# Biases on another queue, halves inverted singly, one more piece summed on TensorE: both ends of a norm-attention kernel

## The chip, the cores and the metric

One core of one Trainium2 chip runs the whole program. The metric is the device time of one execution in microseconds (us). The median of six runs of the kernel before is 1860.31 us (1860.1 to 1861.24).

## The reference

The input `x` is 32 images of 256 channels on 32 by 32 positions, in float32. Each image is group-normed (32 groups of 8 channels), projected to q, k and v, put through attention with 8 heads of 32 channels over the 1024 positions with a strictly causal mask, and added to `x`:

```python
def _L0_conv_ref(x, q_w, q_b, kv_w, kv_b):
    xf = x.reshape(B, C, S)
    q = jnp.einsum('oc,bcs->bos', q_w, xf) + q_b[None, :, None]
    kv = jnp.einsum('oc,bcs->bos', kv_w, xf) + kv_b[None, :, None]
    ...
    mask = jnp.tril(jnp.ones((S, S), dtype=x.dtype), -int(MASK_CENTER))
    scores = jnp.einsum('bhqd,bhkd->bhqk', q, k) / jnp.sqrt(jnp.asarray(dk, x.dtype))
    scores = jnp.where(mask == 0, jnp.asarray(-10000.0, x.dtype), scores)
    attn = jax.nn.softmax(scores, axis=-1)
    attn = jnp.where(mask == 0, jnp.asarray(0.0, x.dtype), attn)
    out = jnp.einsum('bhqk,bhkd->bhqd', attn, v)
...
x = x + _L0_conv_ref(_gn(x), L0_conv_q_w, L0_conv_q_b, L0_conv_kv_w, L0_conv_kv_b)
```

## The kernel before, in words

The images ("batches", 0 to 31) are worked one after the other, all in float32. The 256 channels are two groups `g` of 128 partitions, and each group holds four heads. The 1024 positions are two halves `hf` of 512 columns. A batch so has four outputs of 128 by 512, which the code numbers n = 0 to 3 (n = 2 g + hf) and which I call its halves.

**Norm and projection.** `norm_channels`, `norm_mean`, `norm_deviation`, `norm_variance`, `norm_rstd` and `norm_apply` make the normed `xn`: statistics on VectorE (DVE), averages over the groups by small products on TensorE (PE), the power on GpSimd (POOL), and the subtraction and scaling of one half per call on DVE. `project_qk` multiplies on PE into a PSUM tile, and ScalarE (ACT) writes q or k with the bias `qk_bias` added (line 230). For q the bias has to be scaled first (line 565). `project_v` makes v without its bias, which is added at the very end.

**Visits.** Attention of a batch goes in N = 12 visits, six for each group. A visit is a pair of pieces: a piece `f[hf][k]` is one block of 128 keys against the queries of a half; `h[k, part]` is one against half of such queries. `scores` (line 297) makes the products of both pieces on PE into three PSUM tiles, ACT takes three exponentials into `e` and `eh` (lines 330 and 332), and POOL sets masked entries to zero (line 290). One visit later `values` (line 343) multiplies the exponentials with v into `acc` and, where `summed` is true, DVE adds them into the running total of the half (line 359). ACT copies the finished `acc` to `num` (line 362).

**Sums.** A total still has to be summed over the 128 partitions. For batches 0 to 29 that goes through DMAs that fold it. For the last two ("late") batches `sums` (line 409) does it with `sum_keys` on PE into `pd`, ACT copies `pd` to `den`, and a DMA writes four rows to the DRAM tile `sums`. For the last half of batch 31 some pieces skip the total: `sum_piece` (line 396) adds them into `pd` on PE, and `sum_total` adds the total of the rest.

**Inverting and finishing.** `gather` (line 432) reads the sums back into a tile `rows` spread over partitions, `check_sums` (line 439) marks on DVE whether they are in range, `invert` (line 445) takes the reciprocal on DVE, writes it to the DRAM tile `inverses` and reads it back, broadcast over the 32 channels of each head, into one tile `rb` for each half (line 453, allocated in line 459 with four buffers). `finish` (line 462) multiplies `num` with `rb`, adds the bias of v and `x` on DVE and sends the half out (line 470). `finish_aside` (line 472) does the same with two operations on POOL and one on ACT. Halves 2 and 3 of the last batch take no detour through DRAM: `check_here` (line 484) and `invert_here` (line 491) work on the sums where they are, and `end_last` (line 495) closes with half 3 in two parts.

**Order.** The loop in lines 618 to 637 runs over all visits `i`. For each it emits the scores of visit `i`, then the functions that `at[i]` holds, then the values of visit `i - 1`, then the functions of `after[i]`. (Where `i % 12` is 6, those of `at[i]` go between the exponentials of that visit.) `when` (line 530) puts a function into one of these lists; lines 584 to 617 do so for each batch, with `first = 12 b`. On PE, ACT, DVE and POOL the order is exactly the order of this code (`manual_schedule`, line 554). SyncE (SP), which issues nearly all DMAs, is not in that list: its order is the compiler's choice. Each engine and each queue of DMA issues works in its order, and waits there for whatever the next instruction needs.

**What sets the last batch's order.** Sums of halves 0 to 3 are made behind visits 3, 7, 9 and 12 (`SUMS`, line 549, and line 593). Batch 30 is finished behind visits 7, 7, 8 and 9 of batch 31 (`FINISH`, line 551), and its inverses are asked for in visit 4 (lines 603 to 606).

Of the kernel before, what the change touches and what calls it, by code (L numbers as in the profile page):

```python
# [17 lines left out]
P = 128  # L18
HD = 32
CPG = 8  # L20
HALF = 512
# [6 lines left out]
ROW = 64  # L28
# [3 lines left out]
def tile_norm_attention_residual(  # L32
# [19 lines left out]
    nc = tc.nc  # L52
    B, C, H, W = x.shape
    S = H * W
# [54 lines left out]
    def unshifted():  # L109
# [24 lines left out]
        def load_weights():  # L134
            for n, w in enumerate((q_w, kv_w[0:C], kv_w[C : 2 * C])):
                live["wn", n] = epool.tile([P, 4, HALFBANK], F32, tag="eh", bufs=4, name=f"wn_{n}")[:, :NG, :C]
                nc.sync.dma_start(out=live["wn", n], in_=w.rearrange("(o p) c -> p o c", p=P))
            nc.scalar.dma_start(out=qk_bias[:, 0, :], in_=q_b.rearrange("(g p) -> p g", p=P))
            nc.scalar.dma_start(out=qk_bias[:, 1, :], in_=kv_b[0:C].rearrange("(g p) -> p g", p=P))
            nc.scalar.dma_start(out=v_bias_col, in_=kv_b[C : 2 * C].rearrange("(g p) -> p g", p=P))  # L140

        def turn_weights(n):
            wn = live["wn", n]
# [64 lines left out]
        def norm_apply(b, cols):  # L208
            if cols.start == 0:
                live["xn", b] = work.tile([P, NG, S], F32, tag="xn", name=f"xn_{b}")  # L210
            mean, rstd = live["mean", b], live["rstd", b]
            for g in range(NG):
                nc.vector.tensor_scalar(
                    live["xn", b][:, g, cols], live["x", b][:, g, cols],
                    mean[:, g : g + 1], rstd[:, g : g + 1], ALU.subtract, ALU.mult,
                )
# [215 lines left out]
        def gather(b, ns):  # L432

            if ns.start == 0:
                live["rows", b] = small.tile([P, ROW], F32, tag="rows", name=f"rows_{b}")
            part = slice(ns.start * HD, ns.stop * HD)
            nc.sync.dma_start(out=live["rows", b][part], in_=spread_rows(live["sums", b])[part])

        def check_sums(b, ns):
            part = slice(ns.start * HD, ns.stop * HD)  # L440
            rows, ok = live["rows", b][part], in_range[part, :ROW]
            nc.vector.scalar_tensor_tensor(ok, rows, SUM_MIN, ok, ALU.is_ge, ALU.mult)  # L442
            nc.vector.scalar_tensor_tensor(ok, rows, SUM_MAX, ok, ALU.is_le, ALU.mult)  # L443

        def invert(b, ns):
            part = slice(ns.start * HD, ns.stop * HD)
            inv = small.tile([P, ROW], F32, tag="inv", name=f"inv_{b}_{ns.start}")
            nc.vector.reciprocal(inv[part], live["rows", b][part])  # L448
            live["inv", b] = dram.tile([4, 4, HALF], F32, tag="inv", name=f"inverses_{b}_{ns.start}")
            nc.sync.dma_start(out=spread_rows(live["inv", b])[part], in_=inv[part])  # L450
            by_half = live["inv", b] if b >= B - 2 else live["inv", b].rearrange("j n c -> n j c")
            for n in ns:
                nc.sync.dma_start(
                    out=inverses(b, n),
                    in_=by_half[n].unsqueeze(1).broadcast_to([4, HD, HALF]),
                )
# [27 lines left out]
        def check_here(n, ok):  # L484

            least = small.tile([P, 1], F32, tag="least", name=f"least_{n}")
            junk = small.tile([P, HALF], F32, tag="den", name=f"junk_{n}")
            nc.vector.tensor_scalar(junk, live["den", n], SUM_MIN, 1.0, ALU.is_ge, ALU.min, accum_out=least)  # L488
            nc.vector.scalar_tensor_tensor(ok, live["most", n], SUM_MAX, least, ALU.is_le, ALU.mult)
# [40 lines left out]
        def when(i, f, where=at):  # L530
            where.setdefault(i, []).append(f)
# [22 lines left out]
        with tc.manual_schedule(engines={ENG.PE, ENG.Activation, ENG.DVE, ENG.Pool}):  # L554


            load_weights()
            if B > 1:
                load(1)
            junk = small.tile([P, 1], F32, tag="most", name="junk")  # L560
            nc.scalar.activation(junk, ones, AF.Exp)
            keep_busy(11)
            for g in range(NG):
                norm_channels(0, g)
            nc.vector.tensor_scalar_mul(qk_bias[:, 0, :], qk_bias[:, 0, :], SCALE)
            norm_mean(0)
            keep_busy(3)
            norm_deviation(0)
            norm_variance(0)
            norm_rstd(0)  # L570
            for n in range(3):
                turn_weights(n)
            keep_busy(3)
            for hf in range(NH):
                norm_apply(0, slice(hf * HALF, (hf + 1) * HALF))
            units = projections(0)
            for n, f in zip((None, None, 0, 0, 0, 0) + PROJECT[6:], units):
                if n is None:
                    f()
                else:  # L580
                    when(n, f)
            if B > 1:
                prepare(1, (None, None, 0, 1, 2, 3, 3, 3))
            for b in range(B):
                first, last, late = b * N, b == B - 1, b >= B - 2
                if b >= 1:
                    for n, f in zip(PROJECT if not last else PROJECT[:-1] + (8,), projections(b)):
                        when(first + n, f)
                if b >= 2:
                    when(max(first - 2 * N + 6, 0), lambda b=b: load(b))  # L590
                    prepare(b, [first + n for n in PREPARE])
                for n in every:
                    v = first + (N if last and n == 3 else SUMS[n])
                    if late:
                        when(v, lambda b=b, n=n: sums(b, *divmod(n, NH)), after)
                    else:
                        when(v, lambda b=b, n=n: fold(b, n, 2 * HD), after)
                        when(v + 2, lambda b=b, n=n: fold(b, n, HD), after)
                        when(v + 4, lambda b=b, n=n: stack(b, n))
                if not last:  # L600
                    if not late:
                        when(first + N + 6, lambda b=b: sum_folded(b), after)
                    v = first + N + (2 if late else 8)
                    when(v, lambda b=b: gather(b, every))
                    when(v + 2, lambda b=b: check_sums(b, every))
                    when(v + 2, lambda b=b: invert(b, every))
                    for n in every:
                        when(first + FINISH[late][n], lambda b=b, n=n: finish(b, n), after)
                else:
                    when(first + N - 4, lambda b=b: gather(b, every[:2]))  # L610
                    when(first + N - 3, lambda b=b: check_sums(b, every[:2]))
                    when(first + N - 3, lambda b=b: invert(b, every[:2]))
                    when(first + N, lambda b=b: check_here(2, in_range[:, ROW : ROW + 1]))
                    when(first + N, lambda b=b: invert_here(b, 2, slice(0, HALF)))
                    when(first + N, lambda b=b: finish(b, 2))
                    for n in every[:2]:
                        when(first + N, lambda b=b, n=n: finish_aside(b, n), after)
            for i in range(B * N + 1):
                if i < B * N:

                    between = at.pop(i, ()) if i % N == 6 else ()
                    scores(i // N, *visits[i % N], between)
                for f in at.pop(i, ()):
                    f()
                for n, pc in enumerate(products[(i - 1) % N] if i else ()):

                    summed = i < B * N - 2 or (i == B * N - 2 and n == 0)
                    values((i - 1) // N, pc, summed)
                    if i == B * N:
                        sum_piece(B - 1, pc, stop=n == 1)  # L630
                        if n == 0:
                            sum_total(B - 1)
                if i == B * N - 1:
                    for n, pc in enumerate(products[N - 2] + products[N - 3][1:]):
                        sum_piece(B - 1, pc, start=n == 0)
                for f in after.pop(i, ()):
                    f()
            assert not at and not after
            outside = end_last(B - 1)
# [157 lines left out]
```

## Time and profile before

| what | value |
|---|---|
| median of six runs | 1860.31 us (1860.1 to 1861.24) |
| time of the profiled execution | 1860.07 us |
| its span, first to last instruction | 1858.0 us |
| granted TensorE clock, mean | 0.997 |
| busy ACT, share of the span | 1413.9 us, 76% |
| busy POOL, share of the span | 773.4 us, 42% |
| first projection on PE | 13.47 us after the start |
| issue of the last output DMA | 1853.56 us after the start |

The times in a line of the timeline are the start of a group of like instructions on one engine and the time that the group takes, in us from the start of the span; in brackets stands the idle time of that engine just before, and what ended it. "SPq" and "ACTq" are the queues that issue DMAs, "PEld" is the loading of weights on PE. The chain of waits gives start, time, engine, tile and line of the work that led to the end. A row of the stretch table gives start and end of a stretch, its length, then busy time (with the number of instructions) of PE, PEld, DVE, ACT and POOL, the granted clock of PE, the mean busy share of the sixteen DMA engines, and GB/s. A PE instruction in such a line is one pass; a product of float32 operands has two.

The stretches of the last batch by the scores of its visits: visit 4 starts at 1808.40 us, visit 8 at 1825.59, visit 11 at 1836.96. The last product of the attention ends at 1846.31 us.

### The profile page before, as it was taken

What the parts mean: (1) busy time and instruction counts of PE and PEld (TensorE: products, weight loads), DVE (VectorE), ACT (ScalarE), POOL (GpSimd) and SP (SyncE); (2) the same over time, 40 slices, a digit from 0 to 9 for tenths busy, and PEclk for the clock granted to TensorE, in tenths of its full rate; (3) what the DMA queues carried; (4) which work ended last, traced back from release to release, by engine and by line L of the source; (5) the groups of instructions that cost most, each with busy time, mean ns of one, the idle gap of its engine ahead of it and who ended that gap; (6) DMA issues with size and microseconds to landing.
All of it is one profiled execution on the core that took longest, in us unless ns stands there. A gap on an engine that the chain in (4) does not pass through costs nothing. (4 is left out here: it accounts for less than half of the span.)

```text
span 1858.0 us, 54181 instructions
## 1 busy us (share of the span) xinstructions
PE 1839.9 (99%) x23440; PEld 933.9 (50%) x23440; DVE 1555.9 (84%) x1601; ACT 1413.9 (76%) x1777; POOL 773.4 (42%) x743
## 2 busy tenths in 40 slices
PE   8999999999999999999999999999999999999997
PEld 5455555454554555545555545555455555454543
DVE  3778888888888888888888888888888888888868
ACT  5777777777777777777777777777777777777776
POOL 1443443434434444344344343443443443434314
PEclk9999999999999999999999999999999999999999
DMA  3447665676766676666767656767567666667412
GB/s 120 69 79 145 140 147 112 116 146 138 144 116 127 133 142 140 134 124 124 140 139 143 122 119 131 145 141 144 108 126 146 138 141 114 130 132 141 98 45 89
DMA packets 77517, 233.43 MB, mean 126 GB/s; under 512 B 19808, under 2 KB 20832, under 8 KB 61912
## 3 DMA queue, kind: packets, MB, share of 16 engines
q0 software_dynamic: 15360, 94.39, 36.7%
q1 hardware_dynamic: 61096, 135.51, 24.6%
q8 instruction: 186, 3.05, 0.7%
q14 instruction: 59, 0.48, 0.1%
q10 hardware_dynamic: 816, 0.00, 0.0%
HBM read 68.41 MB, written 35.62 MB: 56 GB/s over the span
## 5 line engine op out<-in xcount | busy, mean ns | idle before, releaser
L332 ACT ACTIVATE e<-sT 128x1024 f32<-128x1024 f32 x768 | 747.9, 1022 | 357.2 <-PE sT L276 302.7
L359 DVE TENSOR_TENSOR e<-e,eh 128x1024 f32<-128x1024 f32 x381 | 523.8, 1389 | 262.3 <-PE acc L354 188.6
L359 DVE TENSOR_TENSOR e<-e,e 128x1536 f32<-128x1536 f32 x381 | 629.3, 1652 | 15.4 <-POOL e L290 1.0
L290 POOL TENSOR_SCALAR_AFFINE_SELECT e<-e 128x512 f32<-128x512 f32 (+1 forms) x256 | 367.6, 1436 | 622.9 <-ACT e L332 600.3
L276 PE MATMUL sT<-q,k 32*128 32x256 f32 (+3 forms) x7168 | 606.3, 458 | 0.8 <-ACT k L230 0.8
L276 PEld LDWEIGHTS sT<-q,k 32*128 32x128 f32 x7168 | 443.9, 184 | 170.1 <-ACT eh L330 65.6
L168 PE MATMUL pp<-xn,wT 128*32 128x512 f32 x4096 | 492.2, 598 | 0.0
L354 PE MATMUL acc<-e,v 128*32 128x512 f32 (+2 forms) x4096 | 400.7, 486 | 0.2 <-POOL e L290 0.2
L330 ACT ACTIVATE eh<-sT 128x1024 f32<-128x1024 f32 x384 | 396.3, 1032 | 0.0
L372 POOL DMA_DIRECT2D e<-e x240 | 199.4, 892 | 397.4 <-PE sT L276 149.9
L168 PE MATMUL ppv<-wT,xn 128*32 128x256 f32 x4096 | 247.3, 382 | 0.0
L354 PEld LDWEIGHTS acc<-e,v 128*32 128x32 f32 x4096 | 132.5, 110 | 223.7 <-issue 200.2
L354 PE MATMUL acc<-eh,v 128*32 128x256 f32 x3072 | 224.4, 379 | 0.0
L168 PEld LDWEIGHTS pp<-xn,wT 128*32 128x32 f32 x4096 | 107.0, 109 | 219.5 <-issue 197.2
L354 PEld LDWEIGHTS acc<-eh,v 128*32 128x32 f32 x3072 | 98.4, 110 | 165.0 <-issue 152.9
L168 PEld LDWEIGHTS ppv<-wT,xn 128*32 128x32 f32 x4096 | 120.2, 109 | 102.5 <-issue 32.1
L290 POOL TENSOR_SCALAR_AFFINE_SELECT eh<-eh 128x512 f32<-128x512 f32 x128 | 164.7, 1287 | 0.1
L467 DVE SCALAR_TENSOR_TENSOR rb<-rb,v_bias_col,x 128x512 f32<-128x512 f32 x126 | 95.9, 761 | 4.5
L230 ACT ACTIVATE k<-pp,qk_bias 128x512 f32<-128x512 f32 x128 | 89.4, 698 | 13.5 <-PE pp L168 12.3
L230 ACT ACTIVATE q<-pp,qk_bias 128x512 f32<-128x512 f32 x128 | 89.8, 701 | 2.1 <-PE pp L168 2.1
L466 DVE TENSOR_TENSOR rb<-num,rb 128x512 f32<-128x512 f32 x126 | 87.8, 697 | 0.1
L178 DVE BATCH_NORM_STATS2 st<-x 128x6 f32<-128x512 f32 x128 | 81.8, 681 | 5.3 <-DMA x<-in_x_dram 5.3
(70 smaller groups left out, 535.5 us busy)
## 6 DMA issues: line engine op xcount, KB each, us to landing
e<-e POOLq DMA_DIRECT2D x120, 512.0 KB, 7.9
x<-in_x_dram SPq DMA_DIRECT2D x64, 512.0 KB
out_dram<-rb SPq DMA_DIRECT2D x127, 256.0 KB
rb<-inverses SPq DMA_DIRECT2D x126, 256.0 KB
e<-e POOLq DMA_DIRECT2D x120, 256.0 KB, 4.6
folded<-e SPq DMA_DIRECT2D x120, 256.0 KB
rows<-sums SPq DMA_DIRECT2D x31, 32.0 KB
inverses<-inv SPq DMA_DIRECT2D x31, 32.0 KB
```

Source lines behind the costliest of these rows:

```text
L168: nc.tensor.matmul(out[part], lhsT=lhsT[:, part], rhs=rhs, start=start, stop=stop, skip_group_check=True)
L178: nc.vector.bn_stats(st[:, c, :], live["x", b][:, g, c * HALF : (c + 1) * HALF])
L230: nc.scalar.activation(live[key][:, cols], pp, AF.Identity, bias=qk_bias[:, n, g : g + 1], scale=(SCALE, 1.0)[n],)
L276: return nc.tensor.matmul(pair[:, cols], lhsT=live["k", b, g][rows, kb * P : (kb + 1) * P], rhs=live["q", b, g][rows, hf * HALF + of.start ...
L290: nc.gpsimd.affine_select(out=diagonal, in_=diagonal, pattern=[[0, 4], [0, n], [1, P]], compare_op=ALU.is_gt, fill=0.0, base=0, channel_mu ...
L330: exp = nc.scalar.activation(eh.rearrange("p (n bank) q -> p bank n q", n=2), short, AF.Exp)
L332: nc.scalar.activation(e[:, 2 * a : 2 * a + 2, :], pairs[a], AF.Exp)
L354: nc.tensor.matmul(acc[HD * j : HD * (j + 1), of], lhsT=live["v", b][:, kb, h * HD : (h + 1) * HD], rhs=e[:, j, cols], start=first, stop=l ...
L359: nc.vector.tensor_add(total[:, :, of], total[:, :, of], e[:, :, cols])
L372: nc.gpsimd.dma_start(out=total[:rows], in_=total[rows : 2 * rows], accum_op=ALU.add)
L466: nc.vector.tensor_mul(rb, num[:, within], rb)
L467: nc.vector.scalar_tensor_tensor(rb, rb, v_bias_col[:, g : g + 1], xt[:, g, cols], ALU.add, ALU.add)
```

## The change

Three DMAs that load the biases are issued by SP behind the three loads of the weights, where ACT issued them. The scaling of q's bias on DVE moves from behind the channel statistics to between the two halves of `norm_apply`. In the last batch, halves 0 and 1 are gathered, checked and inverted one by one: half 0 with its gather in visit 5, check and inversion in visit 6 and `finish_aside` behind visit 9; half 1 with its gather in visit 8, check and inversion in visit 9 and `finish_aside` behind visit 12. Before, both were gathered in visit 8, inverted in visit 9 and finished aside behind visit 12. Half 2 is checked and inverted in visit 10, where that was in step 12. Both pieces of visit 9 skip the total of the last half; before, only the second did.

```diff
@@ load_weights
-            nc.scalar.dma_start(out=qk_bias[:, 0, :], in_=q_b.rearrange("(g p) -> p g", p=P))
-            nc.scalar.dma_start(out=qk_bias[:, 1, :], in_=kv_b[0:C].rearrange("(g p) -> p g", p=P))
-            nc.scalar.dma_start(out=v_bias_col, in_=kv_b[C : 2 * C].rearrange("(g p) -> p g", p=P))
+            nc.sync.dma_start(out=qk_bias[:, 0, :], in_=q_b.rearrange("(g p) -> p g", p=P))
+            nc.sync.dma_start(out=qk_bias[:, 1, :], in_=kv_b[0:C].rearrange("(g p) -> p g", p=P))
+            nc.sync.dma_start(out=v_bias_col, in_=kv_b[C : 2 * C].rearrange("(g p) -> p g", p=P))
@@ start
             for g in range(NG):
                 norm_channels(0, g)
-            nc.vector.tensor_scalar_mul(qk_bias[:, 0, :], qk_bias[:, 0, :], SCALE)
             norm_mean(0)
...
-            for hf in range(NH):
-                norm_apply(0, slice(hf * HALF, (hf + 1) * HALF))
+            norm_apply(0, slice(0, HALF))
+            nc.vector.tensor_scalar_mul(qk_bias[:, 0, :], qk_bias[:, 0, :], SCALE)
+            norm_apply(0, slice(HALF, S))
@@ last batch
-                    when(first + N - 4, lambda b=b: gather(b, every[:2]))
-                    when(first + N - 3, lambda b=b: check_sums(b, every[:2]))
-                    when(first + N - 3, lambda b=b: invert(b, every[:2]))
-                    when(first + N, lambda b=b: check_here(2, in_range[:, ROW : ROW + 1]))
-                    when(first + N, lambda b=b: invert_here(b, 2, slice(0, HALF)))
+                    for n, i, out_at in ((0, 5, 9), (1, 8, N)):
+                        when(first + i, lambda b=b, n=n: gather(b, every[n : n + 1]))
+                        when(first + i + 1, lambda b=b, n=n: check_sums(b, every[n : n + 1]))
+                        when(first + i + 1, lambda b=b, n=n: invert(b, every[n : n + 1]))
+                        when(first + out_at, lambda b=b, n=n: finish_aside(b, n), after)
+                    when(first + N - 2, lambda b=b: check_here(2, in_range[:, ROW : ROW + 1]))
+                    when(first + N - 2, lambda b=b: invert_here(b, 2, slice(0, HALF)))
                     when(first + N, lambda b=b: finish(b, 2))
-                    for n in every[:2]:
-                        when(first + N, lambda b=b, n=n: finish_aside(b, n), after)
@@ loop
-                    summed = i < B * N - 2 or (i == B * N - 2 and n == 0)
-                    values((i - 1) // N, pc, summed)
+                    values((i - 1) // N, pc, i < B * N - 2)
...
-                    for n, pc in enumerate(products[N - 2] + products[N - 3][1:]):
+                    for n, pc in enumerate(products[N - 2] + products[N - 3]):
                         sum_piece(B - 1, pc, start=n == 0)
```

## The prediction

> **What bounds the kernel now.** I read the page first, then the timeline of the first 19 and the last 50 us, the chain of waits, and the stretch table (busy time by engine, granted clock, DMA share) at both ends.
>
> ```profile
> span 1858.0 us, 54181 instructions
> PE 1839.9 (99%) x23440; PEld 933.9 (50%) x23440; DVE 1555.9 (84%) x1601; ACT 1413.9 (76%) x1777; POOL 773.4 (42%) x743
> ```
>
> PE is busy throughout, so time is to be had or lost where PE waits: before its first projection, and in the last batch. What is gained at the front is carried to the end unchanged. The profiled execution took 1860.07 us, 0.24 below the median of 1860.31; I sum against its span and add the 0.24 at the end.
>
> The front:
>
> ```profile
> 0.81 0.46 ACTq L138 DMA_DIRECT2D qk_bias<-in_L_conv_q_b_dram  x1
> 5.10 1.29 DVE L178 BATCH_NORM_STATS2 st<-x 128x6 f32<-128x512 f32 x2 [5.10 <-DMA x<-in_x_dram]
> 6.86 1.29 DVE L178 BATCH_NORM_STATS2 st<-x 128x6 f32<-128x512 f32 x2 [0.23 <-DMA x<-in_x_dram]
> 8.54 0.24 PE L168 MATMUL pm<-mv,avg 128*32 128x2 f32 x8 [2.06 <-DVE qk_bias L565]
> 9.95 2.82 PE L147 MATMUL wt<-ident,wn 128*128 128x128 f32 x12
> 13.47 3.64 PE L168 MATMUL pp<-xn,wT 128*32 128x512 f32 x32
> ...
> 4.00:5.00 1.00, 1.00 (x7) 1.00 (x6) 0.00 (x0) 0.00 (x0) 0.00 (x0) 1.00 0.69 197
> 10.00:11.00 1.00, 1.00 (x8) 1.00 (x6) 0.00 (x0) 0.26 (x1) 0.52 (x1) 0.50 1.03 410
> ```
>
> The first chunk of x reaches DVE at 5.10, the second at 6.86, and everything up to 13.47 hangs on the second. The last two rows end with the clock, the DMA share and GB/s: while the biases travel beside x, 197 GB/s are moved; later, with the same x chunks alone, 410. PE idles 2.06 us before `pm`, and from 9.4 to 12.8 its clock is 0.50: the twelve transposes start 0.213 us apart, where `keep_busy` at full clock has single starts at 9.034, 9.146 and 9.257, 0.112 apart.
>
> The end. I number the visits of the last batch 0 to 11; their scores start at 1813.06 (visit 5), 1817.71, 1820.85, 1825.59, 1829.81, 1834.03 (10) and 1836.96 (11).
>
> ```profile
> 1806.89 2.36 DVE e L359 x2
> ...
> 1838.36 2.28 DVE e L359
> ...
> 1841.44 3.27 DVE rb L493
> ...
> 1824.59 1.06 PE L391 MATMUL pd<-e,pick 128*32 128x512 f32 x8 [0.22 <-DVE e L359]
> 1845.70 0.61 PE L391 MATMUL pd<-eh,pick 128*32 128x256 f32 x8
> 1835.22 1.94 ACT L332 ACTIVATE e<-sT 128x1024 f32<-128x1024 f32 x2 [0.36 <-PE sT L276]
> 1813.71 2.36 SPq L453 DMA_DIRECT2D rb<-inverses  x4
> 1828.18 1.74 SPq L470 DMA_DIRECT2D out_dram<-rb  x2
> 1818.00:1822.00 4.00, 4.00 (x52) 1.89 (x52) 3.86 (x3) 3.10 (x4) 3.32 (x3) 1.00 0.26 96
> ```
>
> From 1806.89 the chain runs on DVE alone. PE delivers the last sum at 1845.70 + 0.61 = 1846.31, DVE begins to check it at 1848.30: PE is 1.94 us ahead of DVE (0.05 for the signal). At 1824.59, however, PE itself waits for a DVE addition, and ACT has only 0.36 us to spare before visit 10. The last row shows the four broadcasts of batch 30's inverses: a DMA share of 0.26 is four engines of sixteen. From 1815.2 to 1826 they move some 95 GB/s, so one 262 KB broadcast needs 2.8 us.
>
> **The change, part by part.**
>
> *Biases on SP behind the weights.* Three issues of about 0.48 us leave ACT (nothing there waits) and enter SP ahead of batch 1's x. Without them x should run nearer the 410 GB/s row: 1 MB at the 197-332 of those slices ended at about 6.5; the second chunk should then be in at 5.1 and reach DVE at about 5.5. The first chunk at 4.0-4.1 and its 1.45 us on DVE end at 5.55. So `pm` moves by 6.86 - 5.55 = **-1.31**. Bounds: 0 (the slow start is not the biases') to -1.5 (DVE free of both waits). The weights (0.75 MB) then end before 8, ahead of the transposes' new place at 8.64. The biases come last, at about 10; the scaling behind the first half of xn is due at 10.9, and ACT needs it only after the first projection, at 12.9. If they spread over 5 us as now they end near 13, costing up to +0.6. Without that cover each us later is a us lost. Removing the scaling ahead of `dev` gains nothing: DVE waits there for the mean anyway. Batch 1's x is late by some 1 us at DVE; nothing before 24 us asks for it.
>
> *Clock at the front.* With `pm` at 7.2, PE's 2.06 us idle shrinks to 0.75. If the clock then stays at 1.00, twelve transposes save 12 x (0.213 - 0.112) = **-1.2**, and `pp` starts when xn's first half is done (10.9), no longer behind PE's queue. Bounds 0 and -1.2; I take it all, since the only idle stretch ahead of the drop is the one that goes. Front: -2.5.
>
> *Half 0 inverted in visit 6.* A second trio of check, check and reciprocal runs on DVE. The present trio starts at 1833.45 and the next addition at 1834.29: **+0.84**. Queued behind it are the additions that PE's sum of half 1 waits for at 1824.59 (with 0.22 already lost), so PE, then ACT, are late by the whole 0.84. Its gather reads a sum written from 1809.15; SP is free before the broadcasts, so I expect it to be issued ahead of them.
>
> *`finish_aside` of half 0 in visit 9.* This moves two POOL multiplies/adds (1.27 + 1.28), an ACT pass (0.72) with its one-column copy (0.19) and an output DMA ahead of visit 10's exponentials. POOL's next mask and ACT's `e` and `eh` queue behind them, and PE's visit 11 waits for those. The inputs: `rb` has four buffers, and half 0 of batch 31 takes the one that `finish` of batch 30 sends out at 1828.18. With 0.84 that is 1829.0; a 256 KB output shows DMA traffic until 1830.0 (now), so 1830.8; the broadcast goes out behind the second output and the gather, about 1831.3; traffic starts 1.1 us after an issue (1813.71, 1814.8), lasts 2.8, and lands at 1835.5 with the signal. POOL ends at 1838.1, ACT at 1839.1. The exponentials would start at 1835.22 + 0.84 = 1836.06: **+3.05**. Bounds: +0.55 (inputs early; 0.91 of ACT less its 0.36) and +4.3 (POOL slowed by DVE as at 1845.80, 1.71 + 1.59, and 0.5 more in SP's queue). I take 3.05, the sum of the nearest rows.
>
> *A further piece on PE.* DVE loses an addition of 2.28; PE gains eight instructions of 512 columns, 0.86 us by the spacing at 1840.50. Of it, 0.25 was PE's wait at 1842.66: **+0.61**.
>
> *Check and inversion of half 2 earlier* (0.8 + 3.3 us of DVE): now beside PE's visits 10 and 11, for nothing, as PE is the later one. `finish` of half 1 stays where it is, with POOL less crowded.
>
> So PE's last sum moves to 1846.31 + 0.84 + 3.05 + 0.61 = 1850.81. DVE is then idle by 1847 and starts at once: **-1.94**. End: +2.56.
>
> *Clock at the end.* While ACT is held, PE stands for about 2.2 us and again for about 1.2. The 2.06 at the front preceded a stretch at 0.50. A drop would stretch the last PE work by up to 1.7 (half of one 3.4 us stretch); I take half, **+0.8**.
>
> The Trainium skill ("TensorE: Matmul & The Clock Gate", "What's actually happening") has the clock fall after an idle window of about 3.4 us and the window free-running. Here 2.06 us idle, in a window with 1.34 of 3.40 us busy, preceded the 0.50. By the page's rule alone there would be no drop at the end, and the sum would be 0.8 lower.
>
> A rule that speaks against the change: the skill ("DMA: Bandwidth & Descriptors", "Why a DMA increments its semaphore by 16 and not by 1") has a DMA spread over as many engines as divide its outermost dimension, always the lowest-numbered. The 0.26 share agrees for a broadcast of four. By that rule a 32-row gather uses all sixteen engines and stands behind any broadcast issued before it, which would cost the price of the second rival below.
>
> Sum: 1860.07 - 2.5 + 2.56 + 0.8 = 1860.9; with 0.24, **1861.2**.
>
> **The rivals.**
>
> *No hold* (0.15): half 0's broadcast is in before POOL comes to it. For: its sum is ready 20 us earlier. Against: the buffer leaves only at 1829. End = 0.84 + 0.55 + 0.61 - 1.94 = +0.06; time 1860.31 - 2.5 + 0.06 = 1857.9.
>
> *The gather of half 0 is caught by the four broadcasts* (0.20, the slower side). Place: DVE's check in visit 6, wanted at 1819.70. If SP issues it behind 1813.71, its rows on the four engines wait until about 1827.0, and so does DVE: +7.5, handed to PE at 1824.59 whole. For: the code asks for it after the broadcasts. Against: SP already takes issues out of the code's order as they become ready (sums of half 1 before the outputs at 1828.18). It decides as soon as the gather is behind two of the four broadcasts (which end near 1821). 1861.2 + 7.5 = 1868.7.
>
> *The change does what it says* (0.07): no hold, and the trio fits into DVE's slack. -2.5 + 0.61 - 1.94 = -3.8: 1856.5. Against: DVE has no gap from 1806.89 on.
>
> **How the numbers follow.** Forecast 0.58, its own range 1859 to 1864: below, without the clock price and with a short hold; above, without the clock gain (+1.2) and with the long hold. About 0.2%, 3.7 us, is what a measurement can tell from no change, so 1856.6 and 1864.0 divide. Faster: most of the last rival, 0.06. Slower: the gather case, 0.20, and the forecast's tail, 0.07, together 0.27. Within: 0.67. For 8 in 10 the range takes in the no-hold case and half of the gather case: 1857 to 1868.
>
> **What will show it.** Right: the second `x` chunk at DVE near 5.5, `pp` near 11, transposes near 0.11 us; a PE wait for DVE near 1824 of about 1 us; ACT idle some 3 us for POOL's `rb` ahead of visit 10's `e`; DVE idle before the last check, and the chain's end on PE, POOL and ACT. Wrong: DVE waiting for a DMA ahead of line 442 in visit 6 (the gather rival); no ACT wait there (no hold); x still at 6.9. A q activation waiting for `qk_bias` would overturn the front.

## The result and the profile after

| what | before | after |
|---|---|---|
| median | 1860.31 us (40 runs) | 1864.53 us (20 runs) |
| range of the runs | 1858.61 to 1861.68 | 1864.09 to 1866.2 |
| profiled execution, its span | 1860.07, 1858.0 us | 1865.38, 1863.5 us |
| first projection on PE | 13.47 us | 11.00 us |
| exponentials of visit 10 on ACT | 1835.22 us | 1838.85 us |
| last sum on PE ends | 1846.31 us | 1852.89 us |
| DVE begins its last check | 1848.30 us | 1853.75 us |
| issue of the last output | 1853.56 us | 1859.01 us |

After over before is 1.0023, with a 95% interval of 1.0017 to 1.0029: the change makes the kernel slower by about 4.2 us. The runs of one kernel lie some 1.3 us apart in groups (before: near 1858.7, 1860.1 and 1861.4), so a difference of medians well below 1 us is read from the intervals and from single rows, not from the median.

The head of the page of the kernel after, whose busy shares are within one percent of those of before:

```profile
span 1863.5 us, 54203 instructions
PE 1842.9 (99%) x23448; PEld 934.1 (50%) x23448; DVE 1554.5 (83%) x1603; ACT 1413.6 (76%) x1777; POOL 774.1 (42%) x743
```

PE is busy 3.0 us more, most of it time at the lower clock. The front, in the timeline of the kernel after (DVE, then PE):

```profile
4.19 1.29 DVE L178 BATCH_NORM_STATS2 st<-x 128x6 f32<-128x512 f32 x2 [4.19 <-DMA x<-in_x_dram]
5.76 1.29 DVE L178 BATCH_NORM_STATS2 st<-x 128x6 f32<-128x512 f32 x2
...
7.44 0.24 PE L168 MATMUL pm<-mv,avg 128*32 128x2 f32 x8 [0.66 <-DVE mv L179]
...
8.81 1.53 PE L147 MATMUL wt<-ident,wn 128*128 128x128 f32 x12
...
11.00 1.50 PE L168 MATMUL pp<-xn,wT 128*32 128x512 f32 x12
```

DVE no longer waits for the second chunk (the row of 5.76 has no bracket), PE stands 0.66 us instead of 2.06, the twelve transposes take 1.53 instead of 2.82, and the projections begin 2.47 us earlier.

In visit 6, DVE's check of half 0, and PE's sum of half 1 that waits for the addition behind it:

```profile
1817.14 0.69 DVE L442 SCALAR_TENSOR_TENSOR in_range<-rows,in_range 32x64 f32<-32x64 f32 x1
...
1822.91 1.06 PE L391 MATMUL pd<-e,pick 128*32 128x512 f32 x8 [0.44 <-DVE e L359]
```

The sum was at 1824.59; with the front's 2.47 off and the trio's delay on, 0.79 of that lead is gone again. The stretch around visits 9 to 11, first DVE and POOL, then SP, ACT and PE:

```profile
1832.81 2.36 DVE L359 TENSOR_TENSOR e<-e,eh 128x1024 f32<-128x1024 f32 x2
1835.09 1.75 DVE L466 TENSOR_TENSOR rb<-num,rb 128x512 f32<-128x512 f32 x1
1836.88 1.63 DVE L467 SCALAR_TENSOR_TENSOR rb<-rb,v_bias_col,x 128x512 f32<-128x512 f32 x1
...
1833.97 2.32 POOL L477 TENSOR_TENSOR rb<-num,rb 128x512 f32<-128x512 f32 x1 [10.17 <-DMA rb<-inverses]
1836.38 1.59 POOL L478 TENSOR_TENSOR rb<-rb,x 128x512 f32<-128x512 f32 x1
...
1828.82 0.54 SPq L453 DMA_DIRECT2D rb<-inverses  x1
...
1838.00 0.72 ACT L479 ACTIVATE rb<-rb,v_bias_col 128x512 f32<-128x512 f32 x1 [4.83 <-POOL rb L478]
...
1838.85 1.93 ACT L332 ACTIVATE e<-sT 128x1024 f32<-128x1024 f32 x2
...
1839.92 3.90 PE L276 MATMUL sT<-q,k 32*128 32x256 f32 x24 [4.58 <-ACT e L332]
```

Half 0's broadcast is issued at 1828.82 and releases POOL at 1833.97. POOL takes 2.32 and 1.59 us, ACT stands 4.83 us for it, and PE 4.58 us for ACT.

The stretch table behind that, and the start of the last check:

```profile
1838.00:1841.50 3.50, 1.58 (x6) 0.80 (x8) 3.46 (x5) 3.47 (x5) 0.65 (x1) 0.82 0.48 181
1841.50:1845.00 3.50, 3.50 (x28) 2.00 (x28) 2.80 (x5) 1.72 (x3) 0.03 (x1) 0.50 0.01 2
1845.00:1848.50 3.50, 3.50 (x36) 1.15 (x32) 0.00 (x0) 1.33 (x2) 2.99 (x3) 0.70 0.20 75
...
1852.29 0.60 PE L391 MATMUL pd<-eh,pick 128*32 128x256 f32 x8
1853.03 0.60 ACT L421 ACTIVATE den<-pd 128x512 f32<-128x512 f32 x1
1853.75 0.69 DVE L488 TENSOR_SCALAR_CACHE_REDUCE junk<-pd 128x512 f32<-128x512 f32 x1 [9.35 <-ACT den L421]
```

The third column from the right is PE's granted clock. In finer stretches it is 0.50 from 1840.25 to 1847.08, 6.83 us, with PE busy all the time. DVE's check begins 0.86 us behind PE's last sum, and it waits for ACT's pass over the same sums.

### The profile page after: what moved, and what is told of

It is laid out like the page before. It is cut to its first block, busy times and chain, and to the rows that moved or that the text cites. A ratio compares the mean times of both kernels' runs of the same rounds, so it can differ in the third digit from the quotient of the medians.

```text
span 1863.5 us, 54203 instructions
## 1 busy us (share of the span) xinstructions
PE 1842.9 (99%) x23448; PEld 934.1 (50%) x23448; DVE 1554.5 (83%) x1603; ACT 1413.6 (76%) x1777; POOL 774.1 (42%) x743
## 3 DMA queue, kind: packets, MB, share of 16 engines
q8 instruction: 186, 3.05, 0.7%
```

## The experiments

Theory: the early finish of half 0 holds ACT, PE stands, and its clock falls; the other parts together gain a little. Rivals: the trio on DVE in visit 6 or the end costs the time.

**One part of the change alone.** Three kernels are the one before with one part of the diff each: the front (both front hunks), the piece on PE (the hunk "loop"), and halves 0 and 1 gathered and inverted singly, with both finishes left behind visit 12.

Front: 

> The kernel before with the two edits of the front alone (biases on SP behind the weights, the scaling between the halves of norm_apply). My account: the first projection starts at 11.0 us as in the changed kernel instead of 13.47, the shift of 2.47 us stays to the end: 1857.8 us. Rival (the gain is lost on the way, or the front has a part in the loss): 1860.3 us or more.

Piece: 

> The kernel before with the further piece summed on PE alone (no DVE addition of the first piece of visit 9). My account: DVE's queue of additions, the bound of the last batch before, is 2.28 us shorter, but PE's last sum comes 0.61 later and DVE's last check cannot start until ACT's pass over that sum, 0.86 behind it: 1846.31 + 0.61 + 0.86 = 1847.78 against 1848.30, a gain of 0.5 us of the 2.28: 1859.8 us. Rival (the 2.28 us come out in full): 1858.0 us.

Single halves: 

> The kernel before with halves 0 and 1 gathered, checked and inverted one by one (visits 5 and 6, and 8 and 9), both finished aside behind visit 12 as before; no other edit. My account: the second trio on DVE delays everything behind it by 0.8 us, to the end: 1861.1 us, with PE's wait for DVE ahead of half 1's sum 0.8 longer. Rival (the gather is caught behind batch 30's broadcasts): 1867 us; rival (DVE makes it up, since half 0's broadcast comes earlier): 1860.3 us.

| kernel | median | ratio to before (95%) |
|---|---|---|
| front alone | 1858.45 | 0.9991 (0.9982 to 1.0000) |
| piece alone | 1860.21 | 1.0001 (0.9992 to 1.0010) |
| single halves alone | 1860.83 | 1.0002 (0.9993 to 1.0011) |

None of the three is slower by what the interval can show. The front brings PE's last sum forward by 2.89 us (to 1843.42), and the median by only 1.7. The piece lets DVE begin its last check 0.83 us earlier, and the median doesn't move. On PE it costs 0.40 us: from the scores of visit 10 to the last sum PE takes 12.68 us (1833.94 to 1846.62) where it took 12.28. In both, a short DVE instruction is stretched (timeline of DVE, front alone, then piece alone):

```profile
1838.67 1.05 DVE L489 SCALAR_TENSOR_TENSOR in_range<-most,least 128x1 f32<-128x1 f32 x1
```

```profile
1848.21 1.08 DVE L489 SCALAR_TENSOR_TENSOR ok<-most,least 128x1 f32<-128x1 f32 x1
```

These took 0.16 and 0.18 us in the kernel before. Each stands beside a POOL instruction: a mask of 1.10 us from 1838.61, and an addition of 1.26 from 1848.01; each ends with it.

**The early finish taken back.** The kernel after, with half 0 finished behind visit 12:

```diff
-                    for n, i, out_at in ((0, 5, 9), (1, 8, N)):
+                    for n, i, out_at in ((0, 5, N), (1, 8, N)):
```

> The changed kernel with finish_aside of half 0 back behind visit 12 instead of behind visit 9; all else as changed. My account (ACT is held ahead of visit 10 by POOL, which waits for half 0's broadcast, and PE's clock drops in that pause): no wait there, clock 1.00 to the last sum, PE late by 0.78 for the second trio on DVE and 0.61 for the further piece, DVE's last check 0.86 behind PE's last sum; -2.47 + 0.78 + 0.61 + 0.86 - 1.94 = -2.2: 1858.1 us. Rival (inverting the halves singly, or the further piece on PE, is what costs): 1862 us or more.

Measured: 1857.7, ratio to before 0.9987 (0.9978 to 0.9996). ACT's timeline, and the last sum on PE:

```profile
1833.35 1.94 ACT L332 ACTIVATE e<-sT 128x1024 f32<-128x1024 f32 x2 [0.36 <-PE sT L276]
...
1844.23 0.61 PE L391 MATMUL pd<-eh,pick 128*32 128x256 f32 x8
```

The exponentials start 5.50 us earlier than in the kernel after, and the clock stays at 1.00. This one placement takes away 6.8 us: more than the whole loss.

**The same finish with its inverses in time.** The kernel after with a fifth buffer for `rb`, so that half 0's broadcast needn't wait for an output of batch 30:

```diff
-            live["rb", b, n] = work.tile([P, HALF], F32, tag="rb", bufs=4, name=f"rb_{b}_{n}")
+            live["rb", b, n] = work.tile([P, HALF], F32, tag="rb", bufs=5, name=f"rb_{b}_{n}")
```

> The changed kernel with five buffers of rb instead of four, so that half 0's broadcast need not wait for an output of batch 30; the finish behind visit 9 stays. My account: SP can issue the broadcast at about 1823.6, when the inverses have come through behind batch 30's broadcasts; it lands at about 1828, POOL is done before visit 10, ACT is late by its own 0.6 us alone, the clock stays: 1858.7 us. Rival (it is the place of finish_aside on POOL and ACT that costs, whenever its input comes): 1863 to 1864.5 us.

Measured: 1858.05, ratio 0.9989 (0.9980 to 0.9998). SP, POOL and ACT:

```profile
1824.36 0.52 SPq L453 DMA_DIRECT2D rb<-inverses  x1
...
1829.67 1.61 POOL L477 TENSOR_TENSOR rb<-num,rb 128x512 f32<-128x512 f32 x1 [5.97 <-DMA out_dram<-rb]
1831.35 1.60 POOL L478 TENSOR_TENSOR rb<-rb,x 128x512 f32<-128x512 f32 x1
...
1832.98 0.72 ACT L479 ACTIVATE rb<-rb,v_bias_col 128x512 f32<-128x512 f32 x1
1833.74 0.19 ACT L481 COPY rb<-x 128x1 f32<-128x1 f32 x1
1833.84 1.93 ACT L332 ACTIVATE e<-sT 128x1024 f32<-128x1024 f32 x2
```

The issue is 4.46 us earlier, POOL starts 4.30 us earlier, and ACT has no wait ahead of the exponentials. It isn't the early finish as such that costs the time, but its late input: the buffer that `finish` of batch 30 sends out.

**The clock.** The kernel after, with 18 products of the identity (their result isn't used) on PE behind visit 10's work, where it stands:

```diff
+        def busy_aside(n):
+            pt = misc("busy")
+            for _ in range(n):
+                nc.tensor.matmul(pt[:, :P], lhsT=ident, rhs=ident, start=True, stop=True)
...
+                    when(first + N - 2, lambda: busy_aside(18), after)
```

> The changed kernel with 18 products of the identity (results unused) on PE between the values of visit 9 and the scores of visit 11, where PE stands for 4.58 us. The hold of ACT stays as it is. My account: the clock stays at 1.00 through the last pieces, where it was 0.50 from 1840.25 to 1847.08: some 2.3 us less, 1862.2 us, with the same 5 us of ACT waiting for POOL. Rival (the slow last pieces are not the clock's doing, or the clock falls all the same): 1864.5 us.

Measured: 1862.69, ratio 1.0014 (1.0005 to 1.0023). PE's timeline:

```profile
1835.10 4.29 PE L159 MATMUL busy<-ident 128*128 128x128 f32 x36
1839.77 0.70 PE L281 MATMUL sT<-q,k 32*128 32x256 f32 x4 [0.38 <-ACT e L337]
...
1842.66 1.06 PE L359 MATMUL acc<-e,v 128*32 128x512 f32 x8
...
1849.57 0.61 PE L396 MATMUL pd<-eh,pick 128*32 128x256 f32 x8
```

ACT still waits 4.85 us for POOL, but the products behind run at full clock (1.06 us where the kernel after has 1.94). PE's last sum ends at 1850.18 instead of 1852.89. The hold and the fall of the clock are two costs. The second is worth 1.8 us by the medians; by this row it is 2.71, less 0.16 that was there already when ACT was released (exponentials at 1838.69), so 2.55.

**Why the hold is longer than its rows.** First rival: the broadcast lands late because four DMA engines carry it. The kernel after, with half 0's broadcast cut into four of 32 channels:

```diff
+                if (b, n) == (B - 1, 0):
+                    rb = inverses(b, n)
+                    for j in range(4):
+                        nc.sync.dma_start(
+                            out=rb[j * HD : (j + 1) * HD],
+                            in_=by_half[n][j : j + 1].broadcast_to([HD, HALF]),
+                        )
+                    continue
```

> The changed kernel with half 0's broadcast asked for as four DMAs of 32 channels each instead of one DMA of four heads; the finish behind visit 9 stays. My account: the one DMA uses four engines and needs some 2.8 us of transfer, four DMAs of 32 rows use all sixteen; SP takes 1.6 us longer to issue them, so they land at about 1832.2 instead of 1833.8, ACT is held 1.6 us less and PE stands about 3 us instead of 4.6: 1862.9 us if the clock still falls, 1860.6 us if it stays. Rival (the landing time isn't set by the engines, or POOL is what holds): 1864.5 us.

Measured: 1864.98, ratio 1.0026 (1.0016 to 1.0036), no gain. SP and POOL:

```profile
1828.85 1.75 SPq L456 DMA_DIRECT2D rb<-inverses  x4
...
1833.77 2.33 POOL L485 TENSOR_TENSOR rb<-num,rb 128x512 f32<-128x512 f32 x1 [10.16 <-DMA rb<-inverses]
```

Four issues take 1.75 us on SP instead of 0.54, and POOL is released only 0.20 us earlier. The waits that POOL and ACT record for these DMAs end at the same instants on both engines (1833.36, 1833.55, 1833.63), so it is still the arrival that releases POOL. The landing was expected at 1832.2. The trace shows what kept it: from 1831.75 to 1832.75 the mean share of the sixteen DMA engines is between 0.04 and 0.11, so all but one or two of them had done their part, and the last parts of three of the four DMAs landed only at 1833.14 to 1833.52. A 16 KB packet of the queue that fetches instructions (q8) held an engine for 1.65 us from 1830.48; that it was the late one is likely, not shown. No run takes the late part away, so what a faster transfer would be worth remains open.

Second theory: POOL's two instructions are slow because DVE works with two operands beside them. In this kernel DVE checks and inverts half 2 first (a reciprocal has one operand), and only then makes the two additions and finishes half 3 of batch 30:

```diff
-        FINISH = ((N + 13, N + 13, N + 14, N + 15), (N + 7, N + 7, N + 8, N + 9))
+        FINISH = ((N + 13, N + 13, N + 14, N + 15), (N + 7, N + 7, N + 8, N + 10))
...
-                if not first and summed:
+                if not first and summed and (b, g, k, hf) == (B - 1, 1, 1, 1):
+                    live.setdefault("later", []).append((total[:, :, of], e[:, :, cols]))
+                elif not first and summed:
...
+                    when(first + N - 3, lambda b=b: check_here(2, in_range[:, ROW : ROW + 1]), after)
+                    when(first + N - 3, lambda b=b: invert_here(b, 2, slice(0, HALF)), after)
+                    when(first + N - 3, lambda: [nc.vector.tensor_add(t, t, u) for t, u in live.pop("later")], after)
```

> The kernel after, in which DVE's work beside the early finish of half 0 is put in another order: behind the inverses of half 0 it first checks and inverts half 2 (a reciprocal of 3.35 us), and only then makes the two additions of visit 8's pieces and finishes half 3 of batch 30. In the kernel after these additions and products run while POOL multiplies and adds, and POOL takes 2.32 and 1.59 us; in the kernel before it took 1.27 for the same product beside a reciprocal. Theory (two-operand work on DVE slows POOL): POOL starts at 1834.0 as before, takes 1.27 and 1.28, visit 10's exponentials start at 1837.5 instead of 1838.85, PE stands 3.2 us instead of 4.6; 1863.2 if the clock still falls, 1860.9 if it does not. Rival (POOL is slow there for another reason, or another wait ends last): 1864.5.

Its pair has the change of `FINISH` alone:

> The kernel after, with the finish of half 3 of batch 30 one visit later, behind the check and inversion of half 2; the two additions of visit 8's pieces stay where they are. Theory (two-operand work on DVE slows POOL): POOL's product starts beside the additions and ends beside the reciprocal, between 1.27 and 2.32 us, its sum takes 1.28 beside the reciprocal; exponentials near 1838.1, 1863.8, between the kernel after and the other one of this pair. Rival: 1864.5, as the kernel after.

The first of the pair, DVE, POOL, ACT and PE:

```profile
1834.72 3.35 DVE L495 RECIPROCAL rb<-den 128x512 f32<-128x512 f32 x1 [0.83 <-DMA out_dram<-rb]
...
1833.98 1.28 POOL L479 TENSOR_TENSOR rb<-num,rb 128x512 f32<-128x512 f32 x1 [10.37 <-DVE in_range L491]
1835.34 1.26 POOL L480 TENSOR_TENSOR rb<-rb,x 128x512 f32<-128x512 f32 x1
...
1837.49 1.94 ACT L332 ACTIVATE e<-sT 128x1024 f32<-128x1024 f32 x2
...
1838.56 0.70 PE L276 MATMUL sT<-q,k 32*128 32x256 f32 x4 [3.41 <-ACT e L332]
```

The second, POOL and ACT:

```profile
1834.55 1.96 POOL L477 TENSOR_TENSOR rb<-num,rb 128x512 f32<-128x512 f32 x1 [10.55 <-DMA rb<-inverses]
1836.58 1.26 POOL L478 TENSOR_TENSOR rb<-rb,x 128x512 f32<-128x512 f32 x1
...
1838.73 1.93 ACT L332 ACTIVATE e<-sT 128x1024 f32<-128x1024 f32 x2
```

POOL starts at 1833.98 as before, takes 1.28 and 1.26 us, and the exponentials start at 1837.49, as the theory said to 0.01 us. Beside the additions alone the product takes 1.96 us, and the sum beside the reciprocal 1.26. (In the second POOL starts 0.57 us later than in the first, which is why its exponentials miss the expected 1838.1.) So the rows bear the theory out. The times do not follow as expected: 1864.34, ratio 1.0023 (1.0014 to 1.0032), for the first (expected 1863.2 or 1860.9), and 1865.95, ratio 1.0029 (1.0018 to 1.0040), for the second (expected 1863.8). PE still stands 3.41 us, and the clock still falls (0.50 from 1839.4 to 1846.2). The span of the first is 1862.3 against 1863.5, its last sum 1.10 us earlier, and its fastest run is 1862.85 against 1864.09, but the median is lower by only 0.2. How much of the 1.36 us on ACT reaches the time stays open.

**Kernels that leave the early finish out.** The front, the piece, and half 2's check and inversion in visit 10, with the joint gather and inversion of halves 0 and 1 as before:

> The kernel before with the front, the further piece on PE and the earlier check and inversion of half 2, but halves 0 and 1 gathered and inverted together and both finished aside behind visit 12 as before. My account: neither the trio (0.8) nor the hold of ACT; -2.47 + 0.61 + 0.86 - 1.94 = -2.9: 1857.4 us, the least of all variants so far by some 0.3. Rival (inverting singly pays for itself, since POOL has half 0 behind it earlier): 1858 us or more.

The same, with all pieces of the last sums and ACT's pass over them ahead of the last products with v:

```diff
+                if i == B * N:
+                    for n, pc in enumerate(products[N - 1]):
+                        sum_piece(B - 1, pc, stop=n == 1, keep=True)
+                        if n == 0:
+                            sum_total(B - 1)
+                    sums(B - 1, NG - 1, NH - 1)
                 for n, pc in enumerate(products[(i - 1) % N] if i else ()):
                     values((i - 1) // N, pc, i < B * N - 2)
-                    if i == B * N:
-                        sum_piece(B - 1, pc, stop=n == 1)
-                        if n == 0:
-                            sum_total(B - 1)
```

> As the variant with the joint inversion, and in the last step PE makes all pieces of the last half's sum ahead of the products with v, and ACT passes over that sum ahead of its copy of num. My account: in the last step DVE waits for ACT's pass over the sum, and that comes 1.29 (PE) + 0.25 (ACT) us earlier, unless DVE is still busy with half 2: 1.2 to 1.5 us less than the joint variant, about 1856.0 us. Rival (DVE itself is late at that point): as the joint variant, 1857.4 us.

And the same with DVE's check of half 3 ahead of ACT's pass, to take away the wait of 0.86:

```diff
+                    live["den", 3] = live["pd", B - 1]
+                    check_low(3)
                     sums(B - 1, NG - 1, NH - 1)
...
-            check_here(3, ok)
             both = [slice(c * HALFBANK, (c + 1) * HALFBANK) for c in range(2)]
             invert_here(b, 3, both[0])
+            check_here(3, ok)
```

> As the variant with the sums first, and DVE's check of the last sum comes ahead of ACT's pass over it, with the first reciprocal ahead of the combined verdict. My account: DVE no longer waits for ACT (0.8 us) nor the reciprocal for the verdict; POOL, still busy with half 1, takes back part: 0.9 us less than with the sums first, 1855.0 us. Rival (DVE's wait for ACT is not what sets the end): 1855.9 us.

| kernel | median | ratio to before (95%) |
|---|---|---|
| front, piece, early check of half 2 | 1857.11 | 0.9983 (0.9974 to 0.9992) |
| the same, sums first | 1855.92 | 0.9976 (0.9967 to 0.9985) |
| the same, check first | 1855.86 | 0.9978 (0.9969 to 0.9987) |

The first two came as expected; 1855.92 is 4.3 us below the kernel before. The third brought nothing. Its ACT and DVE:

```profile
1843.65 0.60 ACT L421 ACTIVATE den<-pd 128x512 f32<-128x512 f32 x1 [4.26 <-DVE junk L487]
...
1844.38 1.76 DVE L498 RECIPROCAL rb<-pd 128x256 f32<-128x256 f32 x1 [0.68 <-ACT den L421]
```

Now ACT waits for DVE's check, and DVE's reciprocal for ACT's pass. Whichever reads `pd` first, the other comes behind it: the wait is only turned round.

## Why the prediction was off

The median came 3.3 us above the predicted 1861.2. It lies inside the range of 1857 to 1868, 0.5 above the likeliest case's own range, and on the slower side, where 0.27 of the chance stood. That the wide range holds it is in part luck: its upper end took in the gather's case, which didn't come about. The mechanism was the forecast's, but for one wait that it put at 0.05 us and that took 0.86 (DVE's, behind ACT); besides, the hold, the clock and the piece were mis-sized. Against the rows of the profiled run, which lies 0.85 above the median:

| term | predicted | measured |
|---|---|---|
| front (x, and clock) | -2.5 | -2.47 |
| trio of half 0 on DVE | +0.84 | +0.78 |
| hold of ACT | +3.05 | +5.32 |
| piece on PE | +0.61 | +0.40 |
| clock at the end | +0.8 | +2.55 |
| start of the last check | -1.94 | -1.13 |
| sum | +0.86 | +5.45 |

The hold is 1838.85 less 1833.53 (1835.22 - 2.47 + 0.78). The piece and the clock together are 2.95, the growth from the start of visit 10's exponentials to the end of PE's last sum (11.09 to 14.04 us). In the two kernels that have the piece and the full clock, the one with the early finish taken back and the one with the dummy products, that stretch is 11.49; so the piece is 0.40 and the clock 2.55. The start of the check lay 1.99 us behind PE's last sum and now lies 0.86 behind it. The sum is what the check and the last output's issue are later by (1848.30 to 1853.75, 1853.56 to 1859.01); the span grew by 5.5.

*Front: right.* The first chunk reached DVE at 4.19 instead of 5.10, the second is no longer waited for, and the transposes run at full clock. The gain is carried unchanged: DVE's row at 1806.89 stands at 1804.42.

*Trio: right.* It is at 1817.14 on DVE, PE waits 0.44 us for the addition where it waited 0.22, and its sum of half 1 is at 1822.91. SP issued half 0's gather at 1809.94, ahead of the four broadcasts, so the rival of the gather didn't come about.

*Hold: the mechanism right, the size off by 2.27.* The issue was predicted at 1831.3 in the frame of before, 1828.83 less the front; it came at 1828.82. POOL was expected at 1833.03 and started at 1833.97 (0.94 late): I counted 4.2 us from the issue to the landing, 1.1 to the first traffic, 2.8 of transfer and the signal, and it took 5.15. In the trace the first traffic comes 1.33 behind the issue (1830.15), and the last part lands at 1833.75, 3.6 later; towards the end the output issued at 1831.85 is on the engines too (their share is 0.96 and more from 1832.8 to 1833.4). No run takes this part away by itself. POOL was then to need 2.60 and needed 4.00 (1.40 more). ACT's part was 0.13 shorter, and the start that the hold is counted from was 0.06 earlier, for the trio. I had named the slower rows (1.71 and 1.59) as a bound, and taken the faster ones. The run that moved DVE's two-operand work away got back 1.36 of the 1.40.

*Piece: 0.21 too dear.* I took off the 0.25 us for which PE stood at 1842.66; the runs with the piece show that 0.46 of its 0.86 was hidden.

*Clock: the place right, the size off by 1.75.* I took half of one stretch of 3.4 us; it fell for two. The longer hold leaves PE standing 4.58 instead of 2.2 us; but after 3.41 us it fell for two as well. The Trainium skill ("TensorE: Matmul & The Clock Gate", "What's actually happening") lets the clock fall after an idle window of about 3.4 us and come back after a busy one. If a window is half of the 6.83 us at 0.50, the one from 1836.84 to 1840.25 held 0.33 us of work, and the clock fell; the next, to 1843.66, was busy throughout by the trace, and yet the clock stayed at 0.50 for one more. Read as the prediction quoted it, for a window idle throughout, that rule gives no fall here at all.

*Start of the last check: the step that failed is "starts at once".* I allowed 0.05 us behind PE's last sum; it was 0.86, for ACT's pass over the same tile comes first. In the kernel before, DVE was the later one and hid this. The last experiment shows that turning the order round doesn't remove it.

*The rival "no hold"* gave 1857.9, and the two kernels that remove the hold in different ways ran at 1857.7 and 1858.05: the price of the hold, with the clock behind it, was nearly the whole question. (That these agree to 0.2 us is in part luck, since that sum too has DVE's check 0.81 too early and the piece 0.21 too dear.) The buffer of `rb`, which the prediction had named, decides it.

## What to carry to other kernels

Work that is moved ahead of the critical engine's next instruction can cost as much as its last input is late, so follow that input back to the buffer it is written into and to who frees it; here one more buffer turned a loss of 4.2 us into a gain of 2.1. Take a duration from a row with the same neighbour: POOL's product is 1.27 us beside a reciprocal and 2.32 beside additions. When PE is made to stand, price the clock behind the standstill as a cost of its own, and when the bound moves from one engine to another, look for waits that the first one had hidden.

## What the runs showed of the hardware

*POOL and DVE take turns.* In the kernel after, DVE's second addition runs from 1833.96 to 1835.18; POOL's product, begun at 1833.97, ends at 1836.30, 1.27 us (its undisturbed time) behind 1835.03. DVE's product begins at 1835.09 and ends at 1836.85, about 0.55 behind POOL's end, where it takes 0.68 alone. So, to within 0.2 us, neither is merely slower: each stands until the other is done. The same reading fits the two short DVE instructions of 1.05 and 1.08 us, which end with POOL's. Beside a reciprocal of 3.35 us POOL isn't delayed (its sum takes 1.26 in the kernel with DVE's order changed). The Trainium skill ("SBUF — State Buffer", "Who interferes with whom") has a DVE instruction with two SBUF inputs contend with a GpSimd (POOL) instruction that reads SBUF, and calls the ports that they share an exclusive lock; the rows agree.

*Engines' reads of one sum tile.* ACT's and DVE's reads of `pd` never overlapped, in either order (0.86 us between PE's last sum and DVE in the kernel after; ACT 4.26 and DVE 0.68 us waiting in the last experiment). In both orders the trace has the second reader wait for a semaphore of the first, so the program orders them; what the chip would do without that wasn't tried.

*Small transfers beside large ones.* With the three bias loads behind the weights, batch 0's chunks reached DVE 0.91 and at least 1.10 us earlier. Between 4 and 5 us 197 GB/s were moved in the kernel before, while the biases travelled beside x, and 323 in the kernel after. Whether it is the small transfers or the other queue that slows x wasn't separated.
